# Image 0's edge stencils on raw x, ahead of its channel mixing, in a four-layer convolution kernel

## The chip, the cores and the metric

The kernel runs on one core of one Trainium2 chip. The metric is device time in microseconds (us) of one launch, taken as the median of several runs. The core has five engines that run their own instruction streams in order and wait for one another through semaphores: TensorE (PE, matrix products; PEld is its weight load), VectorE (DVE), ScalarE (ACT), GpSimd (POOL) and SyncE (SP). SP and POOL also issue the DMA transfers. Products go to PSUM, a buffer of eight banks of 128 partitions x 512 float32; everything else lives in SBUF (128 partitions).

## The reference

Four layers over `x` of shape (16, 64, 128, 128), float32. Each adds a function of the group-normalized x (`_gn`: 32 groups of two channels, statistics over the image) to x. This case is about the first two; the others only follow.

```
x = x + conv_w . (gram(gn(x)) . gn(x))          # layer 0
x = x + |gx(gn(x))| + |gy(gn(x))|               # layer 1
x = x + conv3x3(shift(gn(x)), W) + b            # layer 2
x = x + clip(batchnorm(conv1x1(conv3x3(gn(x), w_bin))), 0, 255)   # layer 3
```

`gram` is the 64x64 matrix of products of channels, summed over the pixels, divided by H*W. So layer 0, for a given image, is one 64x64 matrix and a bias applied to the channels of every pixel, once the statistics of that image are known. `gx` and `gy` are the two Scharr kernels, applied to each channel by itself with zeros outside the image:

```
kx = [[3, 0, -3], [10, 0, -10], [3, 0, -3]]
ky = [[3, 10, 3], [0, 0, 0], [-3, -10, -3]]
out = abs(gx) + abs(gy)
```

Mixing channels and a stencil over pixels are both linear and act on different axes, so they may be done in either order, up to what the bias does at the borders of the image.

## The kernel before, in words

Every image passes through these stages: `Gram` (the statistics of layer 0: x is laid with image rows on partitions in the tile `xw`, and 128 small products add up the gram matrix `pg`); `gram_chain` (line 387: some twenty small instructions on VectorE, TensorE and GpSimd, in turns, that make of it the mixing matrix `abd` and the coefficients `co` of the next group norm); `Front` (line 624: layers 0 and 1 in eight chunks of 8 + 8 image rows, image halves on the two halves of the partitions); `Layer2` and `Layer3` (the 3x3 convolutions). After the last image the batch norm closes and the outputs are written.

One chunk of `Front` is: load x (SP and POOL, 256 KB each); `mix`: two products a half chunk, x by `abd`, into the PSUM tile `po`; `prepare`: ScalarE normalizes `po` into one of three slots of the padded tile `xh`, with rows copied into the neighbouring slots; `scharr` parts "stencil", "smooth", "slope": six VectorE operations over 128 x 1,024 elements that make gx in `u` and gy in `e`; "abs": two ScalarE activations in place; "x +" and "+ y": two VectorE operations that add x and both, and sum them for the next statistics; "x2 out": two stores to DRAM; "x2 sq": ScalarE's sum of squares.

The program begins with `first_gram` (line 520): image 0 is loaded in eight tiles `x_first`, turned by TensorE (`turned`), copied into `xw` half by VectorE and half by ScalarE, and its gram products and chain run by themselves. Meanwhile image 1's rows are loaded (`xr`) and copied into `xw` by ScalarE (`rows_to_columns`, line 512). After that a loop over steps (line 1241) runs everything. Each step walks a list of part names written out by hand (`ORDER`, line 76 for "fill"), and that fixes the order in each engine's stream; nothing is reordered later. `FIRST = 15` is the step that chunk 0 of image 0's Scharr parts falls on; the loop starts two steps before it, for mixing. Image b's front runs eight steps after image b - 1's; layer 2 of image 0 starts at step 25. Until then the lists "fill" and the first of the regular ones hold image 0's front, the first chunks of image 1's, and the gram products of images 1 to 3 (`half`, line 602). `weights_of_layer_3` (three calls) and `other_weights` also fall on these steps.

The lines of the profile name almost always L134, the line of the helper `InOrder` that records every operation; instructions are told apart by tiles.

Of the kernel before, what the change touches and what calls it, by code (L numbers as in the profile page):

```python
# [16 lines left out]
P = 128  # L17
# [56 lines left out]
        "+ y", "x2 out", "b own", "d b", "3",  # L74
    ],
    "fill": [
        "a one", "x", "a own", "mix", "b sum", "rows b", "stencil", "b sq", "x2 sq", "0", "near b", "close",
        "load a", "b one", "smooth", "section", "d b", "slope", "b out", "a c", "a sum", "1", "rows a", "abs",
        "x +", "2", "a sq", "mix b", "a out", "d a", "mean", "load b", "+ y", "wi", "x2 out", "b own", "b c",
        "scale", "3",  # L80
    ],
}
FIRST, LAG = 15, 10
# [87 lines left out]
def tile_kernel(ctx: ExitStack, tc: tile.TileContext, x, cw_h, w2_t, b2, wbin_t, w1_t, b1, gamma, beta, consts, out):  # L171
# [10 lines left out]
    def k(name):  # L182
        return kc[:, AT[name][0]:AT[name][1]]
# [47 lines left out]
        return slice(o * C, (o + 1) * C)  # L231

    last = [1]

    def small_product(dst, wt, src):

# [145 lines left out]
        quick.clear()  # L382


    lead = {}

    def gram_chain(b, pg):

# [128 lines left out]

    rows = []

    def first_gram():  # L520

        pg = ps_g.tile([P, CP, W], F32, tag="g", name="pg_0")[:, 0, 0:C + 1]
        src = []

        t = sv("sd")
        dve.memset(t, 1.0)
        act.activation(t, t, AF.Sqrt)
        for m in range(NS):
            t = ring.tile([P, 2, CP, W], F32, tag="x3", name=f"x_first_{m}", bufs=NS + 2)
            t = t.rearrange("p a j w -> p (a j w)")  # L530
            sp.dma_start(t, x[0].rearrange("c (h r) w -> (c h) (r w)", h=2)[:, m * R * W:(m + 1) * R * W])
            src.append(t)
        for m in range(NS + 1):
            if m < NS:
                two = ps_two.tile([P, 2, CP, W], F32, tag="two", name=f"turned_{m}").rearrange("p a j w -> p (a j) w")
                for j in range(R):
                    pe.transpose(two[:, j], src[m][:, j * P:(j + 1) * P], k("I"))
                for j, copy in ((0, dve.tensor_copy), (R // 2, act.copy)):
                    copy(
                        xw[:, m * R + j:m * R + j + R // 2, 0:C, :].rearrange("p w c t -> p w (c t)"),  # L540
                        two[:, j:j + R // 2],
                    )
            if m > 0:
                for w in range(2 * R * (m - 1), 2 * R * m):
                    gram_product(pg, w, 0, W)
        run(Front, 0, Front.first, "x")
        live[Front, 0].load(1)

        for m in range(NS):
            t = ring.tile([P, C // 8, W], F32, tag="x3", name=f"xr_1_{m}", bufs=NS + 2)  # L550
            sp.dma_start(t, x[1].rearrange("c h w -> h c w")[:, m * C // 8:(m + 1) * C // 8, :])
            rows.append(t)
        for link, _ in enumerate(gram_chain(0, pg)):
            if link in (2, 3, 4, 5, 6):
                rows_to_columns(1, link - 2, rows[link - 2])

    class Gram:
        first, last = 1, NS + 2

        def __init__(self, b):  # L560
            self.b, self.xr, self.w, self.parts = b, {}, 0, 0
# [40 lines left out]
        def half(self, r):  # L602

            if self.b == 2 and r == 0:
                for m in range(3):
                    self.load(m)

            m = {3: 0, 4: 1, 5: 2, 7: 3, 8: 4, 9: 5, 11: 6, 12: 7}.get(r)
            if self.b > 1 and m is not None:
                rows_to_columns(self.b, m, self.xr.pop(m))  # L610

                if m + 3 < NS:
                    self.load(m + 3)
                elif self.b < FAST:
                    live.setdefault((Gram, self.b + 1), Gram(self.b + 1)).load(m + 3 - NS)
            self.part({14: 44, 16: 42, 18: 42}.get(r - (self.b == 1), 0))
            if r - (self.b == 1) == 19:
                chains.append(gram_chain(self.b, self.pg))


    lo, hi = slice(0, C), slice(C, P)
    coefs2, coefs3 = {}, {}

    class Front:
# [38 lines left out]
                    mixed.append((self.po[i, g][cols(h)], self.abd[cols(g), cols(g)], t[cols(g), h], True, True))  # L663

        def mix(self, i, g):
            if self.b == 0 and (i, g) in ((0, 1), (1, 0)):

                po = ps_two.tile([P, 2, CP, W], F32, tag="two", name=f"po_0_{i}_{g}")[:, 0]
            else:
                po = ps_po.tile([P, CP, W], F32, tag="po", name=f"po_{self.b}_{i}_{g}")  # L670
            small_product(po, self.abd, self.xs[i][:, g * CP:(g + 1) * CP, :])
            self.po[i, g] = po

# [93 lines left out]
        def store(self, i, t):  # L767
            d = planes(x2_d[self.b])
            for s in range(2):
# [2 lines left out]
                    t.rearrange("p (j s) w -> p s j w", s=2)[:, s],  # L772
                )


    def by_parity(t):

# [348 lines left out]
            pass  # L1126


    live = {}

    def stage_of(stage, b):
        if (stage, b) not in live:
            live[stage, b] = stage(b)
# [2 lines left out]
    def run(stage, b, i, q):  # L1136
        if 0 <= b < B and stage.first <= i <= stage.last:
            stage_of(stage, b).at(i, q)
# [99 lines left out]

    v_again = deque()

    for step in range(FIRST - 2, steps):
        now[0] = step
        (before, j), (stage, i), (after, k2), (later, l) = (planned(step + d) for d in (-1, 0, 1, 2))
        fronts = [b for b in range(B) if Front.first <= step - FIRST - NS * b <= Front.last]
# [37 lines left out]
        for name in ORDER[kind_of(step)]:  # L1282
# [19 lines left out]
                    live.setdefault((Gram, b), Gram(b)).half(4 * (step - at) + q)  # L1302

            first = FIRST
            if step == first and q < 3:
                rows_to_columns(1, NS - 3 + q, rows[NS - 3 + q])
            if q == 1 and first + 2 <= step < first + 5:
                weights_of_layer_3(step - first - 2)
            if q == 1 and step == first + 5:
                other_weights()  # L1310
            tick()
# [181 lines left out]
```

## Time and profile before

| what | value |
|---|---|
| median of 3 runs | 2514.33 us (2512.59 to 2514.65) |
| the profiled execution's own time | 2513.39 us |
| its span, first to last instruction | 2511.6 us |
| TensorE busy | 2409.6 us (96%) |
| VectorE busy | 2078.0 us (83%) |
| ScalarE busy | 2083.6 us (83%) |
| GpSimd busy | 699.5 us (28%) |
| mean granted TensorE clock | 0.974 |
| DMA | 585.35 MB, mean 233 GB/s |

Busy time is the time in which an engine had an instruction at work. A digit of a slice is the busy share in tenths, 9 for 90% and more; `PEclk` is the TensorE clock that was granted, in tenths of full speed. In the timeline a row is: start, length, engine, line, operation, written tile `<-` read tiles, shape, how many; a bracket behind it gives the idle time before it and who ended that. Rows of an engine can overlap by some hundredths, as one operation's end lies over the next one's start. In the chain of waits a row is start, length and what the end of the program was waiting for at that time. An average over the span hides stages: the first 163 us have other limits than the rest.

### The profile page before, as it was taken

Reading aid. Unit: us, or ns where it says so; the run is one execution under the profiler, and the core shown is the slowest. Engines: PE = TensorE matmul, PEld = TensorE weight load, DVE = VectorE, ACT = ScalarE, POOL = GpSimd, SP = SyncE. Lnnn points to the kernel's source line nnn. Section 1 sums busy time; section 2 is a strip of 40 time slices with the busy share of each in tenths; the row PEclk is TensorE's granted clock in tenths of the full one; section 3 lists DMA queues with packets and bytes.
Section 4 is the critical chain, followed back from the end, with each engine's and each line's share of the span. In section 5 each row is a group of like instructions: output and inputs, shape, how many; then the busy total and the mean of one; then the engine's idle time right before and its main releaser. Section 6 shows DMA issues by size and latency. Waiting matters only on the chain.

```text
span 2511.6 us, 52876 instructions
## 1 busy us (share of the span) xinstructions
PE 2409.6 (96%) x19286; PEld 936.2 (37%) x19286; DVE 2078.0 (83%) x2811; ACT 2083.6 (83%) x3509; POOL 699.5 (28%) x1254
## 2 busy tenths in 40 slices
PE   7588999999999999999999999999999999999996
PEld 5333343334334343434343434343333332333332
DVE  4998999999999999999999999999999534444333
ACT  4777999999898898898989899988898656778775
POOL 3251313131423232323323232323232201222222
PEclk8688999999999999999999999999999999999998
DMA  8777888887868686858686978786877798999998
GB/s 229 196 191 205 217 221 224 220 221 197 189 178 199 166 210 163 210 160 207 165 212 183 240 202 233 203 214 160 212 188 174 181 257 277 418 417 418 417 410 338
DMA packets 610579, 585.35 MB, mean 233 GB/s; under 512 B 48480, under 2 KB 521984, under 8 KB 610320
## 3 DMA queue, kind: packets, MB, share of 16 engines
q1 hardware_dynamic: 556752, 425.34, 60.6%
q0 software_dynamic: 53568, 156.63, 20.6%
q8 instruction: 153, 2.51, 0.4%
q14 instruction: 106, 0.87, 0.1%
HBM read 321.46 MB, written 243.28 MB: 225 GB/s over the span
## 4 chain that ended last, share of the span: by engine, by line
PE 77%; DMA 9%; DVE 8%; ACT 2%; issue 2%; POOL 1%; SPq 1%; DVEq 0%; ACTq 0%; POOLq 0%
PE two L134 35%; PE one L134 23%; PE two_again L134 9%; PE bank L134 5%; PE po L134 4%; DVE u L134 3%; DMA end_x<-x_d 3%; DVE e L134 2%; DMA xw<-x_d 1%; DMA v<-x_d 1%; PE pg L134 1%; DMA end_e<-x_d 1%; DMA dA<-x_d 1%; DMA xw<-y_d 1%; DMA xh<-x_d 1%
## 5 line engine op out<-in xcount | busy, mean ns | idle before, releaser
L134 PE MATMUL two<-dA,w 64*64 64x512 f32 (+2 forms) x2304 | 532.8, 595 | 0.0
L134 PE MATMUL two_again<-v_again,w 64*64 64x508 f32 (+1 forms) x3456 | 375.5, 593 | 10.3 <-ACT v_again L134 10.3
L134 PE MATMUL one<-v,w 128*64 128x508 f32 (+2 forms) x1600 | 360.4, 583 | 0.3 <-ACT c L134 0.3
L134 PE MATMUL two<-dB,w 64*64 64x512 f32 (+2 forms) x1536 | 354.6, 594 | 0.0
L134 POOL DMA_DIRECT2D v<-x_d x480 | 238.2, 502 | 399.2 <-PE bank L134 143.7
L134 PE MATMUL one<-v,wi 128*64 128x508 f32 (+3 forms) x1536 | 344.1, 581 | 0.7 <-ACT c L134 0.6
L134 DVE SCALAR_TENSOR_TENSOR e<-e 128x1032 f32<-128x1032 f32 (+1 forms) x256 | 312.8, 1222 | 0.0
L134 ACT ACTIVATE xh<-po,co 128x128 f32<-128x128 f32 (+1 forms) x480 | 274.9, 623 | 25.1 <-PE po L134 24.9
L134 PEld LDWEIGHTS two<-dA,w 64*64 64x64 f32 (+1 forms) x2304 | 150.3, 133 | 287.9 <-issue 283.8
L134 PEld LDWEIGHTS two_again<-v_again,w 64*64 64x64 f32 x3456 | 127.3, 134 | 257.8 <-issue 239.0
L134 ACT ACTIVATE v<-x,co 128x1024 f32<-128x1024 f32 (+3 forms) x256 | 205.3, 847 | 4.0 <-POOL co L134 4.0
L134 PE MATMUL po<-x,abd 64*64 64x512 f32 (+1 forms) x1024 | 179.4, 621 | 21.1 <-ACT xh L134 19.0
L134 PEld LDWEIGHTS one<-v,w 128*64 128x64 f32 x1600 | 109.7, 137 | 211.5 <-issue 187.3
L134 POOL DMA_DIRECT2D q<-dB x128 | 66.6, 522 | 425.4 <-PE one L134 110.9
L134 PEld LDWEIGHTS one<-v,wi 128*64 128x64 f32 x1536 | 103.9, 135 | 215.5 <-issue 171.3
L134 DVE SCALAR_TENSOR_TENSOR y<-two,c 128x1024 f32<-128x1024 f32 x128 | 155.9, 1218 | 32.8 <-PE two L134 23.1
L134 ACT ACTIVATE v<-v,co 128x1154 f32<-128x1154 f32 x128 | 172.0, 1344 | 13.3 <-DMA v<-x_d 11.0
L134 DVE TENSOR_TENSOR dB<-v 128x1024 f32<-128x1024 f32 (+1 forms) x128 | 151.9, 1187 | 36.5 <-ACT v L134 30.9
L134 PE MATMUL two<-q,cross 64*64 64x512 f32 (+1 forms) x768 | 177.2, 570 | 2.2 <-DMA q<-dB 1.5
L134 PE MATMUL two<-dA,wi 128*64 128x508 f32 (+1 forms) x768 | 174.9, 589 | 0.0
L134 DVE TENSOR_TENSOR dA<-v 128x1024 f32<-128x1024 f32 x128 | 156.1, 1219 | 19.3 <-ACT v L134 18.0
L134 DVE SCALAR_TENSOR_TENSOR u<-e,co,u 128x1024 f32<-128x1024 f32 x128 | 164.1, 1282 | 5.3 <-DVE u L134 0.5
(228 smaller groups left out, 4331.4 us busy)
## 6 DMA issues: line engine op xcount, KB each, us to landing
x_d<-u SPq DMA_DIRECT2D x256, 256.0 KB, 3.1
x_d<-x SPq DMA_DIRECT2D x490, 128.0 KB, 4.1
xr<-in_x SPq DMA_DIRECT2D x120, 512.0 KB, 5.8
y_d<-y SPq DMA_DIRECT2D x320, 128.0 KB, 3.9
x<-in_x SPq DMA_DIRECT2D x128, 256.0 KB, 4.9
x<-in_x POOLq DMA_DIRECT2D x128, 256.0 KB, 4.8
end_x<-x_d SPq DMA_DIRECT2D x36, 512.0 KB, 18.1
xw<-x_d SPq DMA_DIRECT2D x33, 512.0 KB, 13.5
```

The lines of the kernel that those rows point to most:

```text
L134: return self.tc.keep_in_program_order(call(*args, **kwargs))
```

## The change

Image 0 gets a front of its own, `FirstFront`. The gradients are taken of raw x, by VectorE, in small pieces that are handed out one after another (`go_on`) between the steps of the first statistics; then gx, gy and x are mixed by `abd`, each as four 64x64 products (`quarters`), and the border terms that the bias makes are added by tiny products with the diagonal of the bias (`diag`) and prepared tiles (`sides`, `line`). ScalarE takes the absolute values straight from PSUM with the scale of the norm.

For this image 0 is loaded once, in another layout: tile m holds four rows from each quarter of the image, the quarters g on the partition halves and h inside; each tile is two loads, all on SP, and six loads of border rows stand ahead of them. The copies of the turned tiles all go to ScalarE. The layer-3 weights and the copies of image 1's rows move into `first_gram`. The mixed gradients need room for chunks that are not mixed yet: eleven slots in tiles that are free then (`kept`). Stores of image 0 are four a chunk. The step loop starts at `FIRST`, image 1's gram parts come three parts earlier in the list, and the list "fill" has a new order. The rest of the program is the same.

```
     "fill": [
+        "rows b", "x", "a one", "stencil", "a own", "abs", "0", "smooth", "b sum", "x +", "b sq", "near b",
+        "mix", "close", "x2 sq", "+ y", "b one", "section", "d b", "b out", "rows a", "slope", "a c", "a sum",
...
     def first_gram():
-        for m in range(NS):
-            t = ring.tile([P, 2, CP, W], F32, tag="x3", name=f"x_first_{m}", bufs=NS + 2)
-            sp.dma_start(t, x[0].rearrange("c (h r) w -> (c h) (r w)", h=2)[:, m * R * W:(m + 1) * R * W])
+        front = live[Front, 0] = FirstFront()
...
-                for j, copy in ((0, dve.tensor_copy), (R // 2, act.copy)):
-                    copy(
-                        xw[:, m * R + j:m * R + j + R // 2, 0:C, :].rearrange("p w c t -> p w (c t)"),
+                for j in (0, R // 2):
+                    act.copy(
+                        xw[:, m * R + j:m * R + j + R // 2, 0:C, :].rearrange("p w c t -> p w t c"),
...
+            if m > 1:
+                front.go_on(5)
+            if 3 <= m < 6:
+                weights_of_layer_3(m - 3)
...
+        for m in range(5):
+            row_load(m)
         for link, _ in enumerate(gram_chain(0, pg)):
+            front.go_on(1)
+            if link < NS:
+                rows_to_columns(1, link, rows[link])
+                if 2 <= link < 5:
+                    row_load(link + 3)
+        front.mix_slopes(0)
...
-            self.part({14: 44, 16: 42, 18: 42}.get(r - (self.b == 1), 0))
+            self.part({14: 44, 16: 42, 18: 42}.get(r + 2 * (self.b == 1), 0))
...
+    class FirstFront(Front):
...
+            for m in range(NS):
+                t = ring.tile([P, 2, CP, W], F32, tag="x3", name=f"x_first_{m}", bufs=NS + 2)
+                for g in range(2):
+                    sp.dma_start(
+                        t[cols(g)].rearrange("p h j w -> p h (j w)"), v[g][:, :, m * CP * W:(m + 1) * CP * W]
+                    )
...
+        def stencils(self):
+            def rows(op, out, t, above, below):
+                for j0, j1 in ((1, CP - 1), (0, 1), (CP - 1, CP)):
+                    after = t[:, :, j0 + 1:j1 + 1] if j1 < CP else below
+                    before = t[:, :, j0 - 1:j1 - 1] if j0 > 0 else above
+                    op(out[:, :, j0:j1], after, before)
+                    yield
+            for i in range(NS):
...
+                yield from rows(dve.tensor_sub, g[:, :, :, 1:1 + W], t, above, below)
+                gy = self.keep(2 * i)
+                dve.tensor_add(gy, g[:, :, :, 0:W], g[:, :, :, 2:W + 2])
+                yield
+                dve.scalar_tensor_tensor(gy, g[:, :, :, 1:1 + W], 10.0 / 3.0, gy, op0=ALU.mult, op1=ALU.add)
+                yield
...
+                yield from rows(dve.tensor_add, s[:, :, :, 1:1 + W], t, above, below)
+                dve.scalar_tensor_tensor(
+                    s[:, :, :, 1:1 + W], t, 10.0 / 3.0, s[:, :, :, 1:1 + W], op0=ALU.mult, op1=ALU.add
+                )
+                yield
+                dve.tensor_sub(self.keep(2 * i + 1), s[:, :, :, 2:W + 2], s[:, :, :, 0:W])
...
+        def quarters(self, dst, wt, src, start=True, stop=True):
+            for g in range(2):
+                for h in range(2):
+                    pe.matmul(
+                        dst(g, h), wt[cols(g), cols(g)], src(g, h), start=start,
+                        stop=stop if isinstance(stop, bool) else stop != (g, h),
+                    )
...
+        def mix_slopes(self, i):
+            if i == 0:
+                self.coefficients_of_first()
...
+            self.quarters(lambda g, h: a[cols(h), g], self.abd, lambda g, h: gx[cols(g), h], stop=False)
+            self.quarters(
+                lambda g, h: a[cols(h), g, :, 0:W:W - 1], self.diag, lambda g, h: self.sides[cols(g), kind, h],
+                start=False,
+            )
+            self.quarters(
+                lambda g, h: b[cols(h), g], self.abd, lambda g, h: gy[cols(g), h],
+                stop=kind == 0 or (kind - 1, kind - 1),
+            )
...
+        def at(self, i, part):
+            if part in ("stencil", "smooth", "slope"):
+                self.go_on(2)
+            if part == "abs":
...
+                        act.activation(
+                            to[:, :, 0:W], t.rearrange("p g j w -> p (g j) w"), AF.Abs, scale=self.co[:, 3:4]
+                        )
...
+                    self.mix_x(i)
...
+                    self.mix_slopes(i + 1)
+            if part == "x +":
...
+                        dve.scalar_tensor_tensor(to, po, self.co[:, 0:1], to, op0=ALU.mult, op1=ALU.add)
...
-    for step in range(FIRST - 2, steps):
+    for step in range(FIRST, steps):
```

## The prediction

> **What bounds the kernel now.** I read the page's slices first, then the windows of the first 300 us, the chain of waits there, and the timeline for single prices.
>
> ```profile
> PE   7588999999999999999999999999999999999996
> DVE  4998999999999999999999999999999534444333
> PEclk8688999999999999999999999999999999999998
> ```
>
> Each digit is one fortieth of the span, 62.8 us. TensorE is full except in the first three and the last. The start is the only place where VectorE is fuller than TensorE. The windows (PE, PEld, DVE, ACT, POOL busy, granted clock, DMA share, GB/s) sharpen that:
>
> ```profile
> 20.00:40.00 20.00, 14.88 (x210) 10.70 (x208) 7.31 (x32) 9.61 (x13) 3.26 (x9) 0.79 1.10 248
> 100.00:120.00 20.00, 11.62 (x194) 7.29 (x190) 19.13 (x25) 14.46 (x22) 4.61 (x6) 0.75 0.77 187
> 120.00:140.00 20.00, 7.23 (x24) 1.69 (x24) 19.73 (x32) 13.66 (x18) 5.98 (x8) 0.50 0.78 192
> 160.00:180.00 20.00, 19.52 (x112) 6.26 (x112) 19.36 (x30) 17.87 (x38) 7.81 (x13) 1.00 0.68 166
> ```
>
> Up to 40 us VectorE is mostly idle; from 43 to 163 us it is the full engine and TensorE waits at a lowered clock; from 163 us TensorE is full. The chain of waits says the same (start, length, what):
>
> ```profile
> 25.62 2.18 PE pg L134 x60
> 27.83 0.24 DVE gs L134
> ...
> 42.86 1.24 DVE u L134
> 44.10 1.15 DVE e L134
> 45.25 1.15 DVE u L134
> ...
> 163.08 2.76 PE two L134 x18
> ```
>
> So the steps of image 0's layer-1 front decide when layer 2 can begin, and with it everything later. Prices, from the timeline:
>
> ```profile
> 44.02 1.24 DVE L134 TENSOR_TENSOR e<-xh 128x1040 f32<-128x1040 f32 x1
> 45.17 1.23 DVE L134 SCALAR_TENSOR_TENSOR u<-xh,u 128x1040 f32<-128x1040 f32 x1
> ...
> 95.57 1.28 DVE L134 SCALAR_TENSOR_TENSOR u<-xh,co,u 128x1024 f32<-128x1024 f32 x1
> ...
> 96.97 1.28 DVE L134 SCALAR_TENSOR_TENSOR u<-e,co,u 128x1024 f32<-128x1024 f32 x1
> ```
>
> A 1,024-column operation takes 1.15 from start to start (44.02 to 45.17); where the next needs its result, 1.40 (95.57 to 96.97) against 1.20 for the same operation with an independent follower (71.70 to 72.90): a direct dependence costs 0.20.
>
> **The handover point.** In the built order of both programs every VectorE instruction from the first stencil of image 1 (the first write of u_1_0) to the end is the same. Before, it starts at 130.19. I work out when it starts after the change; the rest moves with it, for TensorE is full from 33 us later on and its order there is unchanged. The span was 2511.6 and that execution 2513.39; the runs' median is 2514.33, so I add 0.9 at the end.
>
> **The change, part by part.**
>
> *Removed from VectorE:* the eight 0.69 copies of the first statistics (hidden in idle time) and six stencil operations a chunk, 6 x 1.15 = 6.9.
>
> *Added to VectorE, per chunk:* two row operations, each cut into 512, 256 and 256 columns, and four whole ones. Pieces of that size are not in the trace. From 1.15 at 1,024 columns and 0.93 for two starts of 384 (105.65 to 106.58) a line gives 0.60 + 0.33 + 0.33 = 1.26 for a set. Bounds: 1.15 (as one operation) and 1.70 (the 512-column copy's 0.69 and twice the 384-column 0.50). I take 1.26, the line between the nearest rows. A chunk is 2 x 1.26 + 4 x 1.15 = 7.1, eight are 57.0. In the built order 25 of these operations stand directly behind the one they need: 25 x 0.20 = 5.0.
>
> *Moved:* "x +" now reads PSUM in two halves: between 1.20 (one operation) and 1.38 (two 0.69 copies); I take 1.30. With "+ y" (1.21, 51.29 to 52.50) and a dependence it is 2.7 a chunk, 21.7 in all.
>
> *Start.* The first stencil writes into xh, whose clearing on GpSimd ends at 8.13; six border loads now stand ahead of x on SP, at 4.06/8 = 0.51 each, so the first chunk, used at 5.00 before, comes at about 8.1. The third piece needs the second chunk, which came at 8.94 and now comes between that and 12.0; I take 11.2, which lets VectorE wait 2.0. Later chunks are needed 7.9 apart and hide their loads.
>
> *The first statistics.* In the built order 35 stencil operations, three and a half chunks, stand ahead of the copy gs. They take 24.9 and 14 dependences 2.8, so with the start at 8.2 and the 2.0 of waiting gs runs at about 38 instead of 27.83. TensorE's gram product, ScalarE's sixteen copies (0.59 each, 1.2 a chunk against TensorE's cadence of 2.2), the layer-3 weights (0.45 and 0.64, three times) and the eight copies of image 1's rows (1.15 each) all end behind that cover; without it the weights alone would cost 3 us. The chain took 9.8 (27.83 to 37.6), with VectorE busy 5.3 of it; eight stencil operations now fill its waits. Net cost between 5.3 and 9.8; I take 8.0, with the five small coefficient operations in it.
>
> *The rest on VectorE until the handover:* image 1's chain, 5.3 to 9.8 by the same rows, 8.0; the two weight additions 0.9; the first links of image 2's chain 2.0; five operations slowed beside GpSimd's copies (1.38 against 1.23 at 99 to 103), 0.7. Sum: 8.2 + 2.0 + 57.0 + 5.0 + 21.7 + 8.0 + 8.0 + 0.9 + 2.0 + 0.7 = 113.5.
>
> *The tail is not VectorE's.* The last stencil operation ends 7.4 before that sum (two chunks of 2.7, 2.0 of chain), at 106.1. Then TensorE makes gx, gy, the border product and image 1's first product: some 4.7 at a clock of 0.7 (0.86 a pass at full clock). ScalarE's order from there: three writes of xh (0.78 + 0.45 + 0.45), two row copies (2.3), a pair for xh (1.13), the two absolute values (2.1), a row copy (1.15), a square (1.26), another pair (1.13), 10.8 in all, and only then has u_1_0 its rows. 106.1 + 4.7 + 10.8 = 121.6; as part of ScalarE's list can run while TensorE still works, I take 121, 9 us earlier than 130.19.
>
> *Costed at nothing:* the 16 dropped loads of image 0's second copy of x; four stores a chunk instead of two (0.46 each on SP: 0.9 a chunk; a store is waited for only by layer 2's loads, after a coefficient chain of 14 us; uncovered it would cost 2). On SP, image 1's second chunk waits for the tile that the last gx reads, and row loads of image 3 stand behind it; those rows are copied 9 us later, against 5 to 6 us of loading. TensorE has 3 passes a chunk for 2, covered by its 8 idle us in 20.
>
> The Trainium skill, "VectorE: DVE Perf Modes", section "The DRAIN you can't avoid", says a semaphore between consecutive operations costs nothing extra; the trace's 0.20 disagrees, and by the page the sum loses some 6.6 us (an estimate), which is the second case below. The Trainium skill, "SBUF — State Buffer", section "Door 1: the DMA port swizzle", has a load into partitions 0 to 63 reach half the ports; the new half loads would then bring the second chunk about 2 us later still (an estimate from the page), and the sum would be 2 us more; no transfer in the profile shows it alone.
>
> **Forecast:** 2513.4 - 9 + 0.9 = 2505.
>
> **Rivals.**
>
> *Dependences cost nothing and the chains hide fully.* 33 x 0.20 = 6.6 and about 3 of chains go from before the tail; u_1_0 at 112 to 114: 2498. For it: VectorE has other work between links. Against it: 1.40 against 1.20.
>
> *The tail's in-order queues take most.* ScalarE's absolute values stand behind row copies that wait for image 3's rows; two late loads of 2.5 each put u_1_0 at 126: 2510. For it: ScalarE waited 3.0 for such rows before 60 us. Against it: fewer loads compete.
>
> *Slower: TensorE at half clock becomes the bound.* At a clock of 0.50 four passes took 6.37 (36.31), so 1.6 each. Eight chunks of three passes and borders are 42; two gram products of 9.75 (52 to 63.5) at 0.70 are 27 at 0.50; image 1's passes and the chains' small ones 14. TensorE then reaches image 1's first product at about 126 instead of 111, and ScalarE's 10.8 puts u_1_0 at 137: 2521. It decides once TensorE reaches that product later than about 119. For it: 0.50 was granted from 120 to 140. Against it: TensorE was busy 7.2 of 20 there, and where it was busy 19.5 the clock was 1.00.
>
> **How the numbers follow.** Chances: forecast 0.47, dependences free 0.23, tail 0.17, half clock 0.13. The forecast's own range is 2500 to 2509 (5.3 to 9.8 for the two chains, 1.15 to 1.70 for the pieces partly hidden by the tail). The 8-in-10 range takes in the second case with a few us more gain and the third, and stops short of the fourth: 2494 to 2515. About 0.2% (5 us) is what a measurement tells from no change: faster is the forecast but for its edge, the second case and half the third, 0.74; the same 0.14; slower 0.12.
>
> **What would show it.** Right: gs at 36 to 40; 1.26 for a set of pieces; 1.35 between dependent operations; u_1_0 at 117 to 125 behind a write of xh by ScalarE; TensorE full about 9 us earlier. Wrong: VectorE idle for several us between 10 and 105; a set above 1.7; a clock of 0.50 with TensorE full; a gap reopening after 163.

## The result and the profile after

| | before | after |
|---|---|---|
| median | 2514.49 us (4 runs) | 2504.99 us (4 runs, 2503.36 to 2507.5) |
| profiled execution, its span | 2513.39, 2511.6 | 2504.12, 2502.4 |
| image 1's first stencil (first write of u_1_0) | 130.19 | 121.57 |
| TensorE full from | 163.08 | 154.65 |

The ratio of the times is 0.996, its 95% interval 0.9948 to 0.9971: the changed kernel is 9.5 us faster. The span is 9.2 us shorter, and 8.6 of that are there when VectorE begins image 1. Behind it the lead isn't constant: at the first stencils of later chunks it is 4.9 us at 536 us and 7.9 at 1,938, and 9.2 only at the end. "TensorE full from" has an exception as well, which the prediction passed over: before, TensorE was busy 10.8 of the 20 us from 220 to 240, and after, 9.0 of the 20 from 210 to 230.

The slices of the page, 62.6 us each now:

```profile
PE   6798999999999999999999999999999999999996
...
DVE  7899999999999999999999999999999534444333
...
PEclk8898999999999999999999999999999999999998
```

VectorE's first digit is 7 where it was 4, and TensorE's is 6 where it was 7. The windows that the prediction read before (PE, PEld, DVE, ACT, POOL busy, granted clock, DMA share, GB/s):

```profile
20.00:40.00 20.00, 13.23 (x248) 11.41 (x246) 19.55 (x32) 13.42 (x21) 1.62 (x3) 0.94 1.03 231
100.00:120.00 20.00, 14.82 (x210) 7.32 (x204) 13.79 (x31) 14.17 (x18) 2.35 (x5) 0.90 0.87 232
120.00:140.00 20.00, 13.52 (x173) 8.39 (x173) 18.52 (x28) 15.34 (x25) 11.61 (x15) 0.58 0.82 205
160.00:180.00 20.00, 20.00 (x114) 6.68 (x112) 19.70 (x31) 18.61 (x39) 8.69 (x18) 1.00 0.93 217
```

VectorE is full from 20 to 40 us, where it had been busy 7.31. From 100 to 120 it is busy only 13.79 where it had 19.13: the end of image 0 is no longer VectorE's alone. The clock in the first three of these windows, 0.94, 0.90 and 0.58, is higher than before (0.79, 0.75 and 0.50). The chain of waits (start, length, what):

```profile
6.90 5.87 DMA x_first<-in_x
...
12.87 0.44 DVE xh L134
...
57.09 5.55 PE pg L134 x167
...
99.04 5.45 PE pg L134 x165
104.49 1.03 PE po L134 x8
...
106.08 1.14 DVE row_first L134
...
120.40 1.14 ACT xh L134 x2
121.57 1.24 DVE u L134
...
154.65 2.76 PE two L134 x18
```

It leaves VectorE at 51 us for two chunks of TensorE's products and image 1's gram (57.09), and again at 99 for image 2's gram. Both pieces matter below. Between the rows shown it also passes a load of rows (79.30 to 85.02), behind which VectorE did not wait, and stores (111.66 to 116.79), which one of the experiments takes up.

### The profile page after: what moved, and what is told of

Read it like the earlier page. It is cut to its first block, busy times and chain, and to the rows that moved or that the text cites. A ratio compares the mean times of both kernels' runs of the same rounds, so it can differ in the third digit from the quotient of the medians.

```text
span 2502.4 us, 53299 instructions
## 1 busy us (share of the span) xinstructions
PE 2409.0 (96%) x19478; PEld 939.5 (38%) x19478; DVE 2078.4 (83%) x2860; ACT 2076.6 (83%) x3484; POOL 689.3 (28%) x1244
## 3 DMA queue, kind: packets, MB, share of 16 engines
q0 software_dynamic: 52928, 154.53, 20.2%
## 4 chain that ended last, share of the span: by engine, by line
PE 76%; DMA 11%; DVE 7%; ACT 2%; issue 2%; SPq 1%; POOL 0%; DVEq 0%; POOLq 0%; ACTq 0%
PE two L134 36%; PE one L134 23%; PE two_again L134 8%; PE bank L134 4%; PE po L134 4%; DMA end_x<-x_d 3%; DVE u L134 2%; DMA xw<-x_d 1%; DVE e L134 1%; SPq L134 1%; DMA v<-x_d 1%; DMA y_d<-y 1%; DMA end_e<-x_d 1%; DVE xh L134 1%; DMA xw<-y_d 1%
## 5 line engine op out<-in xcount | busy, mean ns | idle before, releaser
L134 DVE SCALAR_TENSOR_TENSOR e<-e 128x1032 f32<-128x1032 f32 x240 | 293.5, 1223 | 0.0
L134 ACT ACTIVATE xh<-po,co 128x128 f32<-128x128 f32 (+1 forms) x450 | 258.7, 625 | 13.8 <-PE po L134 12.7
L134 PEld LDWEIGHTS one<-v,w 128*64 128x64 f32 x1600 | 109.8, 137 | 211.4 <-issue 189.2
L134 ACT ACTIVATE junk<-x 128x1024 bf16<-128x1024 f32 x128 | 134.7, 1052 | 39.6 <-DVE x L134 39.2
L134 DVE SCALAR_TENSOR_TENSOR x<-two,c 128x1024 f32<-128x1024 f32 x128 | 156.8, 1225 | 10.8 <-DVE two L134 0.5
```

The costliest lines, as they stand in the source:

```text
L134: return self.tc.keep_in_program_order(call(*args, **kwargs))
```

## The experiments

The handover to image 1 is set by three moments: when VectorE starts its last whole stencil operation, when TensorE starts the last gx product made of it, and when VectorE starts u_1_0. All in us, from one profiled execution of each; the ratio is to the kernel before on the same chip, with its 95% interval. The changed kernel was timed on one chip only, so medians of two rows from different chips that lie 1 or 2 us apart do not tell the kernels apart.

| kernel | last stencil | last gx | u_1_0 | median | ratio |
|---|---|---|---|---|---|
| the changed kernel | 105.99 | 107.36 | 121.57 | 2504.99 | 0.9960 (0.9948 to 0.9971) |
| e1_after_stats | 128.64 | 130.28 | 144.41 | 2523.98 | 1.0033 (1.0021 to 1.0045) |
| e2_x_ahead | 106.06 | 107.43 | 121.52 | 2505.18 | 0.9954 (0.9940 to 0.9968) |
| e3_interleaved | 105.49 | 106.86 | 120.99 | 2503.82 | 0.9948 (0.9933 to 0.9962) |
| e4_three_u | 107.52 | 108.89 | 123.36 | 2504.12 | 0.9950 (0.9935 to 0.9966) |
| e5_two_queues | 105.32 | 106.69 | 120.78 | 2504.46 | 0.9960 (0.9944 to 0.9975) |
| e6_whole_rows | 104.56 | 106.39 | 120.89 | 2502.69 | one execution |
| e7_inter_slope | 104.80 | 106.59 | 120.72 | 2502.88 | 0.9954 (0.9942 to 0.9967) |
| e8_rows_later | 107.14 | 108.51 | 123.22 | 2506.34 | 0.9968 (0.9956 to 0.9981) |
| e9_gram_back | 105.78 | 108.16 | 122.67 | 2503.53 | 0.9961 (0.9947 to 0.9975) |
| e10_inter_three | 94.16 | 108.10 | 122.25 | 2504.99 | 0.9962 (0.9949 to 0.9974) |
| e11_both | 92.90 | 110.68 | 124.82 | 2507.72 | 0.9972 (0.9961 to 0.9983) |
| e12_gram2_later | 94.21 | 109.41 | 126.32 | 2519.17 | 1.0020 (1.0010 to 1.0031) |

### The early start taken away

```
             if m > 1:
-                front.go_on(5)
+                pass
...
-            front.go_on(1)
             if link < NS:
```

> All stencil operations of image 0 stand behind the first statistics; nothing else is changed. Theory (the early start under the statistics is the gain): gs at about 27.5 instead of 38.5, the coefficients at about 38, and then 80 stencil operations at the 7.6 us a chunk of the changed kernel's trace, 61 us, 2.9 a chunk of additions and 8 of image 1's chain: last stencil operation at about 125 instead of 107, first stencil of image 1 at about 139 instead of 121.6, time about 2522, slower than before. Rival one (the gain is that VectorE has fewer operations, six stencils a chunk fewer and no copies): first stencil of image 1 at 120 to 126, time 2503 to 2509. Rival two (TensorE's and ScalarE's lists set the pace, not VectorE): mixing starts 11 us earlier, first stencil of image 1 at 121 or before, time 2505 or less.

```profile
33.63 0.23 DVE L134 COPY gs<-pg 128x65 f32<-128x65 f32 x1 [31.00 <-PE pg L134]
...
44.42 0.68 DVE L134 TENSOR_TENSOR xh<-x_first 128x512 f32<-128x512 f32 x1
...
144.41 1.24 DVE L134 TENSOR_TENSOR u<-xh 128x1040 f32<-128x1040 f32 x1 [1.32 <-ACT xh L134]
```

Timeline of VectorE in that kernel. The theory held: behind the first statistics the same stencil operations cost 22.8 us at u_1_0 and some 18 in the time (17.8 in the span), and the kernel is then slower than before the change. Having fewer operations on VectorE is by itself no gain; where they stand is. A size was off: gs stands at 33.63, not at 27.5, and u_1_0 at 144.41, not at 139. With nothing else to do VectorE waited 31 us for the gram, which is complete 5.8 us later than the 27.83 of the kernel before. The loads in halves, the copies, now all ScalarE's, and the layer-3 weights among them cost that much together; what each costs was not taken apart. In the changed kernel the stencils cover it. Some 5 us of the 22.8 are lost again by 1,290 us, in steps of under 1 us; why was not followed.

### The order of the first loads

```
-            for h, g, row in ((1, 0, HH - 1), (0, 1, HH // 2 - 1), (1, 1, HH + HH // 2 - 1)):
-                sp.dma_start(self.above[cols(g), h, 0], x[0][:, row, :])
...
                 self.src.append(t)
+                if m == 1:
+                    for h, g, row in ((1, 0, HH - 1), (0, 1, HH // 2 - 1), (1, 1, HH + HH // 2 - 1)):
+                        sp.dma_start(self.above[cols(g), h, 0], x[0][:, row, :])
...
```

> The six border loads are issued behind the first two chunks of x instead of ahead of them. Theory (the late first loads are on the path): first stencil piece at about 8.1 (the clearing of xh ends there) instead of 10.6, the first whole stencil operation at about 11 instead of 13.3, and everything behind it 2 us earlier: gs at 36.5, first stencil of image 1 at about 119.5, time about 2503. Rival (later waits take it up: VectorE waits 0.8, 1.4, 3.0 and 2.4 us for products, ScalarE and stores between 55 and 117): gs earlier but first stencil of image 1 within 0.7 of 121.6, time within 1 of 2505.

The first piece ran at 9.32 instead of 10.57, but the next one then waited 2.38 for the border rows, which had moved behind; the first whole operation came at 13.20 instead of 13.33, gs stood at 38.38 against 38.51, and u_1_0 did not move. So the test was weaker than meant: it exchanged one late load for another.

### The price of a dependence

```
-                yield from rows(dve.tensor_sub, g[:, :, :, 1:1 + W], t, above, below)
-                gy = self.keep(2 * i)
-                dve.tensor_add(gy, g[:, :, :, 0:W], g[:, :, :, 2:W + 2])
+                gy = self.keep(2 * i)
+                yield from rows(dve.tensor_sub, g[:, :, :, 1:1 + W], t, above, below)
+                yield from rows(dve.tensor_add, s[:, :, :, 1:1 + W], t, above, below)
+                dve.tensor_add(gy, g[:, :, :, 0:W], g[:, :, :, 2:W + 2])
...
```

> The same ten stencil operations a chunk in another order, so that none stands directly behind the one that it needs. By 0.12 us a direct dependence (spacing 1.26 against 1.14 in the changed kernel's trace) a chunk takes 7.1 us instead of 7.6 where nothing else stands between, and the last stencil operation ends some 3 us earlier; by the 0.20 of the prediction, 5 us earlier; if a dependence costs nothing (the rival that was put at 2498 rests on that), a chunk still takes 7.6. First stencil of image 1: 118.5 by the first, 116.5 by the second, 121.6 by the third; time 2502, 2500, 2505. If later waits take the gain up, gs moves and the first stencil of image 1 doesn't.

```profile
19.43 0.68 DVE L134 TENSOR_TENSOR xh<-x_first 128x512 f32<-128x512 f32 x1
...
26.52 0.68 DVE L134 TENSOR_TENSOR xh<-x_first 128x512 f32<-128x512 f32 x1
...
54.38 1.41 DVE L134 SCALAR_TENSOR_TENSOR u<-po,co_first,u 128x512 f32<-128x512 f32 x2 [2.08 <-PE po L134]
...
62.85 1.41 DVE L134 SCALAR_TENSOR_TENSOR u<-po,co_first,u 128x512 f32<-128x512 f32 x2 [0.97 <-PE po L134]
```

In the interleaved kernel a chunk's stencils take 26.52 - 19.43 = 7.09 us; in the changed kernel they take 27.12 - 19.52 = 7.60. Four direct dependences are 0.51, so one is 0.13. That part of the expectation held, but not the rest: gs came 2.7 earlier, and u_1_0 only 0.6. Of the 2.7, 1.4 were left at image 0's last coefficient (48.70 against 50.09) and 0.9 at the second addition (62.85 against 63.76). The waits at 54.38 and 62.85, together 0.85 longer than in the changed kernel, say where part of it went: VectorE was early, and TensorE's product po, which the addition needs, was not.

### The pieces of the row operations

```
-                for j0, j1 in ((1, CP - 1), (0, 1), (CP - 1, CP)):
-                    after = t[:, :, j0 + 1:j1 + 1] if j1 < CP else below
-                    before = t[:, :, j0 - 1:j1 - 1] if j0 > 0 else above
-                    op(out[:, :, j0:j1], after, before)
-                    yield
+                op(out[:, :, 0:CP], t, t)
+                yield
+                yield
+                yield
```

> The row operations of image 0's stencils are left as one whole operation each of a tile with itself, so the differences over rows and with them gx and gy of image 0 are left out. Sixteen of the 48 stencil instructions fall to one of 1,024 columns where there were three pieces. By the prediction's 1.26 for a set against 1.15 whole, plus the dependence that it keeps, a chunk takes 7.4 instead of 7.6 us; by the upper bound of 1.70 it would take 6.5. The copy gs then stands at about 36 to 37 (no wait for the second chunk either), the first stencil of image 1 within 1 of 121.6 if the waits for products between 55 and 69 take the gain up as they did with the interleaved order, at 119.5 if VectorE's work alone sets it.

A chunk took 7.32 (17.32 to 24.64 on VectorE's timeline), so two sets of pieces cost 0.28 over whole operations, 0.14 a set. gs moved by 2.9, of which 2.1 were there at the first slope_first (11.25 against 13.33), as the first operation no longer needs the second chunk. u_1_0 moved by 0.7: again VectorE waited for po (2.96 before the addition of chunk 1, where it had been 1.44).

### The stores, costed at nothing

```
-                    self.u = work.tile([P, R, W + 2], F32, tag="u", name=f"u_0_{i}")
+                    self.u = work.tile([P, R, W + 2], F32, tag="u", name=f"u_0_{i}", bufs=3)
...
```

(and the same for the later images, with the room for it)

> Three tiles u instead of two, so that the absolute value of a chunk need not wait for the four stores of the chunk two before. Theory (four stores instead of two, costed at nothing, cost something: ScalarE waited 1.8 us for x_d<-u at 94, and 2.4 us stand before VectorE's addition at 116.8): these two waits go, first stencil of image 1 some 1 to 2.5 us earlier, time 2502.5 to 2504. Rival (VectorE and the order of ScalarE's list set the pace, the stores don't): the waits move to other causes, first stencil of image 1 within 0.7 of 121.6, time within 1 of 2505.

The rival held for the waits. ScalarE's 1.8 before the absolute value of chunk 5 went, and its next wait, for VectorE's addition, was 3.41 instead of 1.47. The wait that the trace puts down to x_d<-u before 116.8 is there still, with another name (2.41, put down to ScalarE's u): a releaser that ended last by some hundredths need not be the cause. From image 1's gs to image 2's, everything took as long as in the changed kernel (70.37 to 108.66 is 38.29, against 38.25 from 68.88 to 107.13), and u_1_0 was not earlier.

It was 1.8 later, where the rival had it within 0.7, and 1.5 of that stand at image 1's gs already. There the clock differs, not the work. The gx products of chunk 1 in the changed kernel, and here:

```profile
54.91 1.20 PE L134 MATMUL gx_first<-row_first,abd 64*64 64x512 f32 x8
```

```profile
55.33 2.27 PE L134 MATMUL gx_first<-row_first,abd 64*64 64x512 f32 x8
```

The granted clock was 1.00 from 54.9 to 56.0 there and 0.50 from 55.3 to 57.0 here, behind the same list of products. The same row is 2.28 in e8_rows_later and 2.22 in e9_gram_back. So the times in the table, from one execution each, can differ by 1 to 1.5 us with no help from the edit.

### Two queues for the half loads

```
-                    sp.dma_start(
+                    (sp, act)[g].dma_start(
```

> The load of each tile of image 0's x into partitions 64 to 127 is issued on ScalarE's queue instead of SP's, so that both halves of a tile are under way together. Before the change one load filled all 128 partitions and the first 25 us moved about 400 GB/s at their height; after it each load fills 64 and the rate stays near 215. Theory (a half load alone is slow, two together aren't): rate again over 300 GB/s from 10 us on, second chunk no later than 1 us behind the first, first gram complete at 31 instead of 33.6; the first whole stencil operation at 11 to 12 instead of 13.3. Rival (256 KB loads are slow by their size or by the 2 KB rows, whatever the queue): rate stays near 215 GB/s, nothing moves. First stencil of image 1: within 0.7 of 121.6 by both, as the run with x ahead of the borders showed that later waits take an earlier start up; time 2504 to 2506.

GB/s in 40 equal slices of the first 25 us: before, after, and with two queues.

```profile
GB/s 0 0 22 181 125 347 408 402 393 401 429 320 221 257 334 413 419 413 406 400 387 329 224 290 360 385 251 204 211 183 220 195 184 176 206 186 196 290 288 305
```

```profile
GB/s 0 0 17 88 144 246 330 402 173 151 159 295 216 229 243 210 252 210 252 216 223 220 210 189 194 198 212 208 190 221 198 207 207 216 220 239 203 233 207 223
```

```profile
GB/s 0 0 18 116 170 293 302 414 365 224 237 280 223 243 216 200 207 197 203 249 226 246 239 202 180 204 204 218 287 251 259 246 193 229 370 371 256 265 348 281
```

From 10 to 13 us (the 17th to the 21st slice) they are 387 to 419 before and 210 to 252 after, with the DMA engines nine tenths busy or more in both. With both halves under way on two queues they are 197 to 249. The first gram was complete at 35.6 instead of 33.6, since ScalarE issued loads until 16.7 before its first copy. The first whole stencil operation came at 12.07 instead of 13.33. So the rival held for the rate, and the time did not move.

### The wait for po moved

```
-        "rows b", "x", "a one", "stencil", "a own", "abs", "0", "smooth", "b sum", "x +", "b sq", "near b",
+        "rows b", "x", "a one", "stencil", "a own", "abs", "0", "smooth", "slope", "b sum", "x +", "b sq", "near b",
```

(on top of the interleaved order; "slope" left out at its old place)

> The interleaved order, and the third pair of stencil operations of each step moved ahead of the addition of the mixed x, which waited 2.1 and 1.0 us for TensorE's product in the interleaved run. Theory (the gain of the interleaving was lost in VectorE's waits for the product behind image 1's gram): these waits shrink to under 0.5, last stencil operation some 2 us earlier than in the interleaved run, first stencil of image 1 at 118.5 to 119.5, time about 2502. Rival (ScalarE's list of row copies and absolute values, tied to the ends of the gram products of images 1 and 2, sets the end of this phase): the waits go, the first stencil of image 1 stays within 0.7 of the interleaved run's 121.0, time within 1 of 2504.

The wait of chunk 0 went, that of chunk 1 grew from 0.97 to 2.97, and gs of image 1 waited 1.74 for the gram product where it had waited 0.79. The rival's number came out (120.72), with TensorE's list as the place instead of ScalarE's. From image 0's coefficients (the last co, 47.9 to 50.3) to image 1's gs it was 18.7 to 20.2 us in the changed kernel and in all nine runs with the early start and image 1's gram in its place, however early VectorE was.

### Image 3's row copies later

```
-        pace[b] = at, 2 if b <= FAST else 1
+        pace[b] = at + (1 if b == FAST else 0), 2 if b <= FAST else 1
```

> Image 3's row copies, its gram product and its chain are planned one step later; nothing else is changed. In the changed kernel's trace ScalarE waits 5.6 us at 98.9 to 104.5 to begin a row copy of image 3, which overwrites what image 2's gram still reads, and the absolute values of chunk 6 stand behind it; three more such copies of 1.1 us stand between there and the first stencil of image 1. Theory (the tail is ScalarE's list, the rival that was put at 2510): without them the first stencil of image 1 comes at 116 to 118 instead of 121.6, time 2499 to 2501, unless the copies are paid for later. Rival (VectorE's order is the bound up to the last stencil operation at 107 and the tail is products and waits of their own): first stencil of image 1 no earlier than 120.5, time 2504 to 2506.

Timelines of TensorE and of ScalarE:

```profile
108.51 1.98 PE L134 MATMUL gx_first<-row_first,abd 64*64 64x512 f32 x8 [1.89 <-DVE gs L134]
```

```profile
113.77 0.78 ACT L134 ACTIVATE xh<-po,co 128x512 f32<-128x512 f32 x1 [5.81 <-PE po L134]
```

The theory's number did not come; the rival's did (123.22, and 2506.34 for 2504 to 2506). ScalarE had one copy less between its first xh and its last (8.3 us from 113.77 to 122.06, against 9.4 from 110.96 to 120.40), but it stood waiting 5.81 for po. The last gx and gy, 1.09 each in the changed kernel, took 1.98 and 1.80 here, at a granted clock of 0.51 from 108.5 to 112. Of the 1.65 by which u_1_0 is later, 1.1 stand at image 1's gs (69.99), behind the slow gx at 55 us, the length of which owes nothing to this edit. So the run says that ScalarE's copies alone do not set the tail, and little about their price.

### Image 1's gram back in its old place

```
-            self.part({14: 44, 16: 42, 18: 42}.get(r + 2 * (self.b == 1), 0))
+            self.part({14: 44, 16: 42, 18: 42}.get(r - (self.b == 1), 0))
```

(and the same for the start of the chain)

> One part of the change undone: image 1's gram parts and the start of its chain come three parts later again, as before the change. In all runs so far the copy gs of image 1 came 18.7 to 20.2 us behind image 0's coefficients, however early VectorE was, and in between TensorE's order is two chunks of products, 43 gram products (5.6 us at 57.0), the x product of chunk 1, and so on. Theory (this stretch of TensorE's order is what VectorE waits for between 54 and 69): with the gram later, the waits of 0.8 and 1.4 for the x products go to under 0.5 and the rest follows 1 to 2 us earlier; first stencil of image 1 at 119.5 to 120.5, time 2502.5 to 2504, if image 1's chain, now about 10 us later (gs at 79 to 81), ends in time. Rival (the earlier gram was a needed part of the change): the chain and its mixing matrix come late, TensorE's order stalls at the chain's links, first stencil of image 1 at 122.5 to 127, time 2506 to 2511.

The wait of chunk 1 for po went, that of chunk 0 stayed (1.16). gs of image 1 came at 69.32, so the 79 to 81 of the expectation was off. The last gx waited for ScalarE, and u_1_0 was 1.1 later, about what the slow gx at 55 us costs; the median is 2503.53. This part of the change is worth nothing that these runs can tell.

### VectorE's stencils done early

```
-                self.go_on(2)
+                self.go_on(3)
```

(on top of the interleaved order of e3_interleaved)

> The interleaved order, and three stencil operations handed out where there were two, so that the last one stands before the addition of chunk 4 instead of that of chunk 6. VectorE then has nothing left of the stencils from about 93 us on, and more of them stand ahead of image 1's copy gs. Theory one (VectorE's sum of work is the bound up to the last stencil operation, as the prediction has it): everything up to there is 3 to 5 us earlier, TensorE's last gx no longer waits 1.9 us for VectorE, and the first stencil of image 1 comes at 115 to 118, time 2498 to 2501. Theory two (TensorE's and ScalarE's lists, with image 2's gram at 99 and its row copies, are as long as VectorE's work): VectorE waits for products and absolute values instead, first stencil of image 1 at 119 to 121.5, time 2502 to 2505. Rival (the early operations delay gs of image 1 and the rest with it): later than 122, time over 2505.

VectorE, TensorE and ScalarE in this kernel:

```profile
94.16 1.21 DVE L134 TENSOR_TENSOR row_first<-xh 128x1024 f32<-128x1024 f32 x1
...
105.90 0.23 DVE L134 COPY gs<-pg 128x65 f32<-128x65 f32 x1 [4.16 <-PE pg L134]
...
122.25 1.24 DVE L134 TENSOR_TENSOR u<-xh 128x1040 f32<-128x1040 f32 x1 [1.32 <-ACT xh L134]
```

```profile
108.10 1.09 PE L134 MATMUL gx_first<-row_first,abd 64*64 64x512 f32 x8 [1.23 <-ACT u L134]
```

```profile
105.90 1.16 ACT L134 COPY xw<-xr 128x1024 f32<-128x1024 f32 x1 [5.56 <-PE pg L134]
106.94 1.11 ACT L134 ACTIVATE u<-gx_first,co_first 128x1024 f32<-128x1024 f32 x1
```

This settles it against theory one, and for the mechanism of theory two. VectorE made its last stencil at 94.16, 11.8 us earlier than in the changed kernel, then waited 4.16 for image 2's gram. TensorE's last gx still stood at 108.10, released by ScalarE's u: the absolute value of chunk 6, which frees the PSUM tile, stood behind a row copy that waited for image 2's gram. u_1_0 was no earlier: 122.25, 0.75 above the range of theory two and just in that of the rival. The rival has a part in it, as image 1's gs came 0.9 later than in the interleaved kernel (68.28 against 67.39).

The edits of e9_gram_back and of this kernel together:

> The two edits together: image 1's gram three parts later, the interleaved order with three operations at a time. By theory one 113 to 116, time 2496 to 2499; by theory two 119 to 121, time 2502 to 2504.5; if the later chain is too late, its links stall TensorE in front of the last chunks' products: over 122.

With image 1's gram in its old place as well, the third case came: u_1_0 at 124.82, image 2's gram ready 2.6 us later than without.

### Images 2 and 3 later

```
-        pace[b] = at, 2 if b <= FAST else 1
+        pace[b] = at + (2 if 1 < b <= FAST else 0), 2 if b <= FAST else 1
```

(on top of e10_inter_three)

> The interleaved order with three operations at a time, and in addition the row copies, gram products and chains of images 2 and 3 planned two steps later. In the run with three operations at a time VectorE had made its last stencil operation 13 us before TensorE took it up, and what stood in between was image 2's gram (5.4 us at 100.4 on TensorE), ScalarE's wait of 5.6 us to begin the first row copy of image 3 behind it, and three more such copies. Theory two (these lists end the phase, not VectorE): with them behind image 1's first products, TensorE's last gx comes at 101 to 103 instead of 108 and the first stencil of image 1 at 113 to 117; time 2496 to 2501 if the moved products fit into TensorE's idle time up to 150, and up to 2505 if they are paid for behind it, where TensorE is full or where image 2's chain is waited for. Theory one (the sum of VectorE's work is the bound): first stencil of image 1 within 1 of 122.

ScalarE and TensorE:

```profile
105.29 1.15 ACT L134 COPY xw<-xr 128x1024 f32<-128x1024 f32 x1 [2.69 <-DMA xr<-in_x]
107.21 1.15 ACT L134 COPY xw<-xr 128x1024 f32<-128x1024 f32 x1 [0.77 <-DMA xr<-in_x]
108.25 1.10 ACT L134 ACTIVATE u<-gx_first,co_first 128x1024 f32<-128x1024 f32 x1
```

```profile
109.41 1.98 PE L134 MATMUL gx_first<-row_first,abd 64*64 64x512 f32 x8 [4.84 <-ACT u L134]
```

A miss. Image 2's gram was gone from that place, but image 2's row copies stood there now, and their loads came late: ScalarE waited 2.69 and 0.77 for them with chunk 6's absolute value behind. The last gx came 1.3 later than without this edit, and took 1.98 at a granted clock of 0.50. TensorE was then busy 23.5 of the 40 us from 120 to 160, against 32.1 in the changed kernel, and did image 3's gram from 164 us on, where it is full. That this is what makes the kernel 14 us slower was not tried. None of these versions is shown to be faster than the changed kernel; the intervals of the best (e3_interleaved and e7_inter_slope) overlap with its own.

## Why the prediction came out, step by step

**The handover.** Right: u_1_0 at 121.57 (121 forecast), behind a write of xh by ScalarE, gs at 38.51, TensorE full 8.4 earlier, no new gap behind it. That the median is 2504.99 where 2505 was forecast is luck: the last stencil came 1.0 later and the tail was 1.1 shorter than in the sum, the handover was 8.6 earlier and not 9, and the end 9.2. "The rest moves with it" held only roughly, as the lead in between fell to 4.9. And TensorE was not full from 163 us on, as the prediction reads: in both kernels it has the gap of some 10 us before 240 us.

```profile
10.57 0.69 DVE L134 TENSOR_TENSOR xh<-x_first 128x512 f32<-128x512 f32 x1 [7.94 <-DMA x_first<-in_x]
...
12.87 0.43 DVE L134 TENSOR_TENSOR xh<-x_first,x_first 128x256 f32<-128x256 f32 x1 [1.27 <-DMA x_first<-in_x]
13.33 1.22 DVE L134 TENSOR_TENSOR slope_first<-xh 128x1024 f32<-128x1024 f32 x1
14.59 1.23 DVE L134 SCALAR_TENSOR_TENSOR slope_first<-xh,slope_first 128x1024 f32<-128x1024 f32 x1
...
22.18 1.23 DVE L134 SCALAR_TENSOR_TENSOR row_first<-xh,row_first 128x1024 f32<-128x1024 f32 x1
23.32 0.69 DVE L134 TENSOR_TENSOR xh<-x_first 128x512 f32<-128x512 f32 x1
...
38.51 0.22 DVE L134 COPY gs<-pg 128x65 f32<-128x65 f32 x1
```

VectorE's timeline in the changed kernel answers to the single prices.

**The start.** Mis-sized: the first piece ran at 10.57, not at 8.2, and the second chunk came at 12.87, not at 11.2. The order of issues was counted, the rate of the half loads was not. By the Trainium skill, "SBUF — State Buffer", section "Door 1: the DMA port swizzle", 64 partitions reach half the ports. The prediction made 2 us of it, outside its sum, and the rate did halve; but two halves on two queues together reach all ports, and the rate stayed low there. So the rule alone does not explain it. What else changed is the length of a row, two rows of 2 KB a partition where it was one of 4 KB; that was not tried by itself.

**Dependences.** Mis-sized: 0.13 us each (e3_interleaved), not 0.20; 25 of them are 3.3, not 5.0. The spacing shows it, 1.26 from 13.33 to 14.59 with a dependence and 1.14 from 22.18 to 23.32 without. The Trainium skill, "VectorE: DVE Perf Modes", section "The DRAIN you can't avoid", has a semaphore between operations cost nothing, measured there on copies; the trace disagrees where the next operation reads the result, by less than the prediction had it.

**Pieces, additions, chain.** A set of pieces is 1.27 (1.26 forecast; 1.13 or 1.14 whole). The additions of a chunk are 2.72 (55.38 to 58.10; 2.7 forecast). Image 0's chain took 12.7 from gs to the first stencil behind the coefficients, with eight stencil operations inside it, some 8 net.

**The sum.** It put the end of the last stencil operation at 106.1, and that came at 107.1. The late start (+1.7) and the waits for po (0.8 and 1.4, which were not in the sum) are 3.9 too much; the cheaper dependences (1.7) and smaller items, such as the slowing beside GpSimd's copies (0.7), which is hardly to be seen here, together took back 2.9. That is luck. And the meaning given to it, that VectorE's order decides up to there, failed. In the changed kernel TensorE's last gx waits for it:

```profile
98.97 5.52 PE L134 MATMUL pg<-xw 128*64 128x65 f32 x168
...
107.36 1.09 PE L134 MATMUL gx_first<-row_first,abd 64*64 64x512 f32 x8 [1.85 <-DVE gs L134]
```

```profile
104.54 1.21 ACT L134 COPY xw<-xr 128x1024 f32<-128x1024 f32 x1 [5.61 <-PE pg L134]
105.61 1.13 ACT L134 ACTIVATE u<-gx_first,co_first 128x1024 f32<-128x1024 f32 x1
...
110.96 0.78 ACT L134 ACTIVATE xh<-po,co 128x512 f32<-128x512 f32 x1 [1.13 <-issue]
...
120.40 1.13 ACT L134 ACTIVATE xh<-po,co 128x512 f32<-128x512 f32 x2 [0.52 <-PE po L134]
```

The wait is 1.85. Where VectorE is ahead of the two other lists (e6, e7, e9, e10, e11), the same product waits 1.23 to 1.29 for ScalarE's absolute value of chunk 6, which stands behind the row copy at 104.54 and so behind image 2's gram. VectorE's list is thus some 0.6 us longer than the list of TensorE and ScalarE beside it, less than what the clock changes from one execution to the next. Two sums of nearly one length hid each other; the prediction had made one.

**The tail.** Right, in its place and nearly in size: from the last stencil's end to u_1_0 it is 14.4, forecast as 4.7 + 10.8 = 15.5. TensorE's part was 3.8 (107.13 to 110.96), as the clock there was 1.00 and not 0.7, and ScalarE's 10.6. One product of the tail did run at half clock: 1.98 from 118.38 at a granted 0.50, 1.03 for the same four records at 109.84, and ScalarE's last pair waited 0.52 for it. From the last gx to u_1_0 it was 14.1 to 14.5 in eleven of the thirteen kernels; the other two (e8, e12) had that gx at half clock.

**Costed at nothing.** The stores: more room for them gained nothing (e4). The slower loads, ScalarE's sixteen copies and the weights were covered, and e1 shows what without: 5.8 us at gs. TensorE's third pass was not covered by its idle time in the way that was said. From 51.3 to 68.3 us the chain of waits lies on TensorE's products of two chunks and image 1's gram, and a lighter VectorE did not shorten the 18.7 to 20.2 us from image 0's coefficients to image 1's gs: it waited for po or for the gram (e3, e6, e7).

**The rivals.** *Dependences free* (2498) would not have come even with the price at zero: e3 and e7 took that cost away in the stencils and gained 0.6 and 0.9 at u_1_0. *The tail's queues* (2510) had the mechanism, ScalarE's values behind row copies, but its two extra waits of 2.5 for rows did not come in the tail (and the 3.0 that the prediction names for it is the sum of four waits of at most 1.3, before 36 us); in e12 such waits did come (2.69 and 0.77), and the last gx stood behind them. *Half clock* (2521) did not come: the clock was 0.63 to 0.97 from 20 to 120 us, and image 1's first product began at 109.8, before the 119 from which it would decide. It cost the 0.5 us at the end of the tail, and e4, e8 and e9 show a microsecond more of it at 55 us.

## What to carry to other kernels

When an engine's work is moved into idle time, add up the other engines' in-order lists to the same handover as well: where two lists end within a us, lightening one gains no more than the difference (here some 0.6 us; of the 11.8 by which VectorE became early in e10, nothing arrived). An idle stretch at the start of a program is worth filling with work that can be done ahead of a long dependence chain, here some 18 us between the same operations placed ahead of it and behind it. And a load that is cut into halves with shorter rows is priced by the rate that it gets, not by its count of issues.

## What the runs showed of the hardware

Loads of 256 KB into 64 partitions in rows of 2 KB moved 210 to 252 GB/s from 10 to 13 us, where loads of 512 KB into 128 partitions in rows of 4 KB had moved 387 to 419, with the DMA engines as busy. A second queue did not bring the rate back (197 to 249, e5).

TensorE's clock after a short pause was not a matter of the pause alone: with 1.85 us of waiting before it the last gx took 1.09 (1.88 and 1.09 in e2), with 1.89 us it took 1.98 (e8), behind the same list of products. At 55 us the gx products of chunk 1 took 1.20 in the changed kernel and 2.27 in e4, and the last pause before them was 0.86 us in both. The Trainium skill, "TensorE: Matmul & The Clock Gate", section "Part 1: The HAM clock gate (the "warmup" mystery)", says that the gate judges TensorE by a window that runs on freely, so that the moment at which the clock changes depends on where in the window the work falls. The runs agree with that, though they do not prove it.
